# Window-attention scores with 49 weight columns in fixed PSUM banks, and the column transform in one piece per half

## The chip, the core and the metric

The kernel runs on one NeuronCore of one Trainium2 chip. Five engines work in parallel, each on its own queue: TensorE (PE, with its weight loads shown apart as PEld), VectorE (DVE), ScalarE (ACT), GpSimd (POOL) and SyncE (SP), which here issues nearly all DMA. The metric is device time in microseconds; a figure for a kernel is the median of its runs. PE writes its results to PSUM, which has eight banks of 128 partitions by 512 fp32 values; DVE and ACT read them from there.

## What is computed

Two layers on a batch of 32 images of 56 x 56 pixels and 128 channels, all in fp32. Each layer adds its result to its input and begins with a group norm (32 groups of 4 channels).

```python
# layer 0: shifted-window attention (windows of 7x7 = 49 tokens, 4 heads of 32)
xs  = roll(gn(x), (-3, -3)); win = windows(xs)              # 64 windows of 49 tokens
q, k, v = split(win @ w_qkv.T); q = q * 32 ** -0.5
attn = softmax(q @ k.T + relative_bias + shift_mask)         # 49 x 49 per head
x = x + roll(unwindow((attn @ v) @ w_proj.T + b_proj), (3, 3))

# layer 1: a Fourier mixer and a feed-forward part
h = gn(x)
xy = idct(einsum(dct(h along w)[:32 modes], w0))             # the rows
xx = idct(einsum(dct(h along h)[:32 modes], w1))             # the columns
x = x + relu((xx + xy) @ W1 + b1) @ W2 + b2
```

## The kernel before

**Cycles.** An image has eight rows of windows. The main loop runs over cycles; each handles one window row of attention, and beside it one step of the Fourier layer of an earlier image. `CONV_BEGIN` is 11: the Fourier layer of an image begins eleven cycles after its attention. Inside a cycle the Fourier step is called c. The order on PE, ACT, DVE and POOL is the order in which the Python code records the instructions (`manual_schedule`); the order on SP is chosen by the scheduler. The first eleven cycles (`first_rows`) have attention alone.

**A steady cycle on PE**, in order: q and k of the window row (L116, through `halved`), a part of the feed-forward input (L116) or of the mixing (L763), the product of the attention weights with v for the row three cycles back (L557, "AV"), a transform of the Fourier layer (L716) where one is due, the scores (L486), the inverse transforms (L802), v (L464), the feed-forward output (L116), and the projection (L602). Scores: for each of four pairs of windows, two pairs of heads and two windows of the pair, one matmul in a 64 x 64 tile of the array. Its weights are q of a window with 64 columns, that is the 49 tokens of the window and 15 that follow; its moving operand is k of two heads, 98 columns. An fp32 matmul stands as two records in the trace. The results lie at partitions 0 and 64 of two banks, one for each pair of heads. DVE adds bias and mask on the way out (L494), finds the maximum (L504), POOL subtracts it, ACT takes the exponential (L511). DVE and ACT empty the AV product (L587, L589).

**PSUM.** `attn_bank` hands out a new tile each time, with the tags pa0 to pa3 in turn, each with one buffer; `conv_bank` hands out new tiles with the tag pc and four buffers. A new tile may be written once all users of the tile before it in the same buffer are done.

**Columns.** The transform along the columns (`transform` with width false) takes tokens that `load_columns` (L745) reads back from a scratch tensor in DRAM, in groups of seven column pairs (`CH`), each group in two DMAs of 56 partitions (one per parity), in a buffer `htok` of which there are two. Groups 0 and 1 are loaded at c = 0, groups 2 and 3 at c = 1 behind the first transform; the transforms are due at c = 1 and c = 2, each with two groups of 224 columns per matmul. The transform along the rows (width true, at c = 0) reads x1 in SBUF, 448 columns per matmul. DVE transposes the results (`turn_modes`, L731).

**Other names.** L151 loads a quarter of the next image in four pieces, L339 to L344 transpose it on DVE; L225 forms bias plus mask (`bm`) at the start, from small tables that POOL loads; L773 stores mixed modes; L820 and L825 empty the inverse transforms.

Of the kernel before, what the change touches and what calls it, by code (L numbers as in the profile page):

```python
# [10 lines left out]
F32 = mybir.dt.float32  # L11
# [4 lines left out]
P = 128  # L16
S = 56
C = 128
# [4 lines left out]
WT = WS * WS  # L23
# [11 lines left out]
JP = 64  # L35
HB = 512

HALVES = (slice(0, P // 2), slice(P // 2, P))
# [10 lines left out]
def swin_fourier_kernel(  # L49
# [20 lines left out]
    nc = tc.nc  # L70
# [4 lines left out]
    work = ctx.enter_context(tc.tile_pool(name="work", bufs=2))  # L75
# [4 lines left out]
    def bank(tag, bufs):  # L80
        return psum.tile([P, HB], F32, tag=tag, name=tag, bufs=bufs)

    turns = count()

    def attn_bank():
        return bank(f"pa{next(turns) % 4}", 1)

    def conv_bank():
        return bank("pc", 4)

# [98 lines left out]
    with nc.allow_non_contiguous_dma(reason="relative position bias, once"):  # L191
# [4 lines left out]
        for ix in range(WS):  # L196
            src = bass.AP(
                rpb_rev.tensor, rpb_rev.offset + WS - 1 - ix, [[span, NH * span], [1, WS]]
            )
# [38 lines left out]
    for ps in LINE:  # L238
        r = ps.start
# [64 lines left out]
    def attn_buffer(r):  # L304
        return a_sb[r % 3 if r < CONV_BEGIN + 4 else r % 2]
# [167 lines left out]
    def attn_scores(im, i, r):  # L473

        q, a = q_sb, attn_buffer(r)

        ps = [attn_bank(), attn_bank()]  # L480
        for pr in range(NP):
            for hp in range(2):
                cs = HALVES[hp]
                for e in range(2):
                    w = 2 * pr + e
                    nc.tensor.matmul(  # L486
                        ps[hp][HALVES[e], pr * 2 * WT : (pr + 1) * 2 * WT],
                        lhsT=q[cs, w * WT : w * WT + JP],
                        rhs=k_sb[cs, :, w],
                        start=True,  # L490
                        stop=True,
                    )
        for hp in range(2):
            nc.vector.tensor_tensor(  # L494
                a[:, 2 * hp : 2 * hp + 2, :, 0:WT].rearrange("p u w j -> p w u j"),
                ps[hp][:, :RT].rearrange("p (w u j) -> p w u j", u=2, j=WT),
                bm[:, i // (NWR - 1), hp],
                ALU.add,
            )
# [43 lines left out]
    def attn_values(im, i, r, both=False):  # L543


        v = v_sb[r % 3]
        po = [attn_bank(), attn_bank()]
        if not both:
            po.reverse()
        HALF = RT // 2  # L550
        po4 = [p[:, :HALF].rearrange("p (r n s) -> p n r s", r=WS, s=WS) for p in po]
        eT = im.eT.pop(i)
        for pr in range(NP):
            for h in range(NH):
                for u in range(2):
                    ks = slice(u * JP, u * JP + WT)
                    nc.tensor.matmul(  # L557
                        po4[u][h * HD : (h + 1) * HD, pr],
                        lhsT=v[ks, pr, h * HD : (h + 1) * HD],
                        rhs=eT[ks, h * NP + pr, :WT],  # L560
                        start=True,
                        stop=True,
                    )

        if i % 2 == 0:
            im.oT = oT_sb[i // 2 % 2]
        oT = im.oT


        oTr = oT[:, i % 2 * RT : (i % 2 + 1) * RT].rearrange("p (r x) -> p r x", x=S)  # L570
        for u in (0, 1) if both else (1, 0):
            src = po[u][:, :HALF].rearrange("p (r f x) -> p r f x", r=WS, f=NP)
            n = NP - u
            dst = bass.AP(
                oTr.tensor,
                oTr[:, :, SS + u * WS :].offset,
                [oTr.ap[0], [S, WS], [2 * WS, n], [1, WS]],
            )
            parts = [(dst, src[:, :, :n])]
            if u:  # L580
                parts += [
                    (oTr[:, :, S - WS + SS :], src[:, :, n, : WS - SS]),
                    (oTr[:, :, 0:SS], src[:, :, n, WS - SS :]),
                ]
            for d, f in parts:
                if u and not both:
                    nc.vector.tensor_scalar(d, f, im.bias[:, 2:3], None, ALU.add)  # L587
                else:
                    nc.scalar.activation(d, f, AF.Identity, bias=im.bias[:, 2:3])  # L589
# [44 lines left out]
    def attn_squares(im, i):  # L634

        n0, n1 = WS * i // 2, WS * (i + 1) // 2
        piece = x1[:, n0:n1]
        im.sq = im.xr.pop(i)[:, : n1 - n0]
        nc.scalar.activation(im.sq, piece, AF.Square, scale=valid)
# [60 lines left out]
    CH = 7  # L700

    def transform(im, width, h):

        if width:
            toks = [x1[:, 2 * CH * h : 2 * CH * (h + 1)]]
        else:
            toks = [im.cols.pop(2 * h + j) for j in range(2)]
        dct_sb = (dct_w if width else dct_h)[:, :, 0]
        py = [conv_bank(), conv_bank()]
        at = 0  # L710
        for tok in toks:
            n = tok.shape[1] * KB
            for g in range(C // KB):
                cs = slice(g * KB, (g + 1) * KB)
                for r, ps in enumerate(LINE):
                    nc.tensor.matmul(  # L716
                        py[r][cs, at : at + n],
                        lhsT=dct_sb[ps],
                        rhs=tok[ps, :, cs],
                        start=True,  # L720
                        stop=True,
                    )
            at += n
        im.py[width, h] = py

    def turn_modes(im, width, h, r):

        p = im.py[width, h][r]
        t = work.tile([P, 4, C], F32, tag="z", name="modes", bufs=4)
        t = t.rearrange("p k c -> p (k c)")[:, : 2 * CH * KB]  # L730
        nc.vector.transpose(t, p[:, : 2 * CH * KB])  # L731
        im.modes.setdefault((width, h), []).append(t)

    def scale_modes(im, width, h, r):

        y = y_of[width][:, : NM * S].rearrange("p (k h n r) -> p h r n k", k=NM, h=2, r=2)[:, h]
        t = im.modes[width, h][r]
        nc.scalar.mul(y[:, r], t.rearrange("p (n k) -> p n k", k=NM), im.rstd)  # L738

    def shift_modes(im, width):  # L740

        y = y_of[width][:, :S]
        nc.scalar.activation(y, y, AF.Identity, bias=im.shift)

    def load_columns(im, g):  # L745

        t = work.tile([P, CH, C], F32, tag="htok", name="htok", bufs=2)
        src = im.scr.rearrange("h (n r) c -> r h n c", r=2)
        for r, ps in enumerate(LINE):
            nc.sync.dma_start(t[ps], src[r, :, CH * g : CH * (g + 1)])  # L750
        im.cols[g] = t

    def mix(im, width, g):

# [169 lines left out]
    def row(r):  # L924
        return (images[r // NWR], r % NWR) if 0 <= r < NB * NWR else (None, 0)

    def fourier(cycle):

        b, c = divmod(cycle - CONV_BEGIN, NWR)
        return [(images[b - k], c + k * NWR) for k in (1, 0) if 0 <= b - k < NB]  # L930
# [18 lines left out]
    def load_first(cycle):  # L949
        for im, c in fourier(cycle):  # L950
            if c == 0:
                load_columns(im, 0)
                load_columns(im, 1)

    def divide(cycle):
        if row(cycle - 1)[0]:
# [80 lines left out]
    def quarters(cycle):  # L1037
        def back():
            for im, c in fourier(cycle):
                for width, g in back_groups(c):  # L1040
                    modes_back(im, width, g)
                    if c < 8:
                        fetch_back(im, width, g)

        if not has_ff(cycle):
            back()
        im, i = row(cycle)
        if im:
            attn_scores(im, i, cycle)
        if has_ff(cycle):  # L1050
            back()

    def eighths(cycle):
        im, i = row(cycle - 3)
        if im:
            attn_values(im, i, cycle - 3, cycle % NWR in VALUES_BY_ACT)
            if cycle % NWR == NWR - 1:
                attn_squares(*row(cycle - 4))
        for im, c in fourier(cycle):
            if c == 0:  # L1060
                for h in range(2):
                    transform(im, True, h)
                    for r in range(2):
                        turn_modes(im, True, h, r)
                next(im.stats)
            if c == 1:
                for r in range(2):
                    scale_modes(im, True, 1, r)
                shift_modes(im, True)
            if c in (1, 2):  # L1070
                transform(im, False, c - 1)
                if c == 1:
                    for g in range(2):
                        load_columns(im, g + 2)

    def last_fetch(cycle):
        for im, c in fourier(cycle):
# [280 lines left out]
```

## Time and profile before

| | us |
|---|---|
| median of 3 runs | 3254.74 |
| the runs | 3251.01, 3254.74, 3256.28 |
| the profiled execution | 3245.75 |
| its span, first to last instruction | 3244.0 |
| mean granted TensorE clock in it | 0.988 of full speed |

The page's costliest groups of PE and their busy time in the profiled execution:

| group | what | records | busy us |
|---|---|---|---|
| L116, wff and hid | feed-forward output | 12288 | 714.1 |
| L116, xf and wff, 512 columns | feed-forward input | 2560 | 578.2 |
| L116, xw and wn | q and k | 2048 | 396.0 |
| L464 | v | 4096 | 291.2 |
| L602 | projection | 3584 | 246.4 |
| L486 | scores | 8192 | 236.2 |
| L557 | AV | 16384 | 208.6 |

A group's line in such a view reads: source line, engine, operation, output and inputs by the program's names, shapes (for PE the tile of the array and then partitions by moving columns), count, busy time, mean duration of one in ns, and the idle time before them with what ended it. Busy time is the union of the durations[...]; the difference between the starts of two matmuls is what the first one costs PE. In the view of one source line the three numbers are the least, median and greatest duration in ns. In the view of waits, a line has the total in us, the number of times and the longest. In the view in order of time, the first number is the start and the second the length, both in us.

### The profile page before, as it was taken

What the parts mean: (1) busy time and instruction counts of PE and PEld (TensorE: products, weight loads), DVE (VectorE), ACT (ScalarE), POOL (GpSimd) and SP (SyncE); (2) the same over time, 40 slices, a digit from 0 to 9 for tenths busy, and PEclk for the clock granted to TensorE, in tenths of its full rate; (3) what the DMA queues carried; (4) which work ended last, traced back from release to release, by engine and by line L of the source; (5) the groups of instructions that cost most, each with busy time, mean ns of one, the idle gap of its engine ahead of it and who ended that gap; (6) DMA issues with size and microseconds to landing.
All of it is one profiled execution on the core that took longest, in us unless ns stands there. A gap on an engine that the chain in (4) does not pass through costs nothing. (4 is left out here: it accounts for less than half of the span.)

```text
span 3244.0 us, 151708 instructions
## 1 busy us (share of the span) xinstructions
PE 3136.1 (97%) x65664; PEld 2363.2 (73%) x65664; DVE 2538.4 (78%) x4787; ACT 2165.5 (67%) x3959; POOL 2343.1 (72%) x2634
## 2 busy tenths in 40 slices
PE   5689999999999999999999999999999999999999
PEld 3467777777777777777777777777777777777776
DVE  8778887878887878888888887878888877887741
ACT  3466776666777666667676776666776666677663
POOL 7777777777777777777777777777777777777741
PEclk8789999999999999999999999999999999999999
DMA  6545556655566656566656556655666656565453
GB/s 113 111 116 147 142 139 145 137 142 139 140 146 146 141 142 144 134 143 148 142 140 147 139 142 145 140 141 144 142 141 148 138 145 144 134 145 139 119 143 96
DMA packets 1173439, 448.46 MB, mean 138 GB/s; under 512 B 529482, under 2 KB 1142908, under 8 KB 1172772
## 3 DMA queue, kind: packets, MB, share of 16 engines
q1 hardware_dynamic: 1163428, 433.22, 56.3%
q8 instruction: 516, 8.45, 1.1%
q10 hardware_dynamic: 8736, 5.38, 0.7%
q14 instruction: 151, 1.24, 0.1%
q0 software_dynamic: 608, 0.17, 0.0%
HBM read 277.00 MB, written 161.48 MB: 135 GB/s over the span
## 5 line engine op out<-in xcount | busy, mean ns | idle before, releaser
L530 POOL TENSOR_TENSOR blocks<-a,rs 128x512 f32<-128x512 f32 x1506 | 1280.0, 857 | 415.1 <-DVE rs L518 291.3
L116 PE MATMUL pc<-xf,wff 128*64 128x512 f32 (+2 forms) x3584 | 714.2, 539 | 1.8 <-DVE xf L820 1.6
L116 PE MATMUL pc<-wff,hid 128*64 128x128 f32 x12288 | 714.1, 273 | 1.7 <-ACT hid L847 1.0
L116 PEld LDWEIGHTS pc<-wff,hid 128*64 128x64 f32 x12288 | 680.4, 137 | 10.3 <-ACT hid L847 5.3
L505 POOL TENSOR_TENSOR a<-a,mx 128x784 f32<-128x784 f32 x251 | 377.7, 1505 | 285.6 <-DVE mx L504 270.2
L116 PEld LDWEIGHTS pc<-xf,wff 128*64 128x64 f32 x3584 | 266.0, 136 | 370.0 <-issue 274.8
L847 ACT ACTIVATE hid<-pc,b1sb 128x512 f32<-128x512 f32 (+2 forms) x896 | 500.5, 643 | 40.9 <-PE pc L116 40.8
L116 PE MATMUL pa<-xw,wn 128*64 128x392 f32 x2048 | 396.0, 501 | 29.8 <-ACT wn L417 29.8
L471 ACT COPY v<-pa 128x512 f32<-128x512 f32 x256 | 151.9, 593 | 349.1 <-PE pa L464 346.2
L494 DVE TENSOR_TENSOR a<-pa,bm 128x392 f32<-128x392 f32 x502 | 260.0, 559 | 152.8 <-PE pa L486 141.6
L451 ACT ACTIVATE k<-pa,bqkv,heads 128x392 f32<-128x392 f32 x512 | 318.9, 674 | 14.7 <-PE pa L116 0.6
L540 DVE STREAM_TRANSPOSE eT<-blocks 128x1024 f32<-128x1024 f32 x256 | 314.2, 1227 | 0.9 <-POOL blocks L530 0.9
L852 POOL TENSOR_TENSOR res<-res,b2sb 128x512 f32<-128x512 f32 (+1 forms) x224 | 252.7, 1128 | 85.1 <-DMA res<-scr 70.8
L438 ACT ACTIVATE q<-pa,bqkv 128x392 f32<-128x392 f32 x256 | 149.8, 585 | 242.6 <-PE pa L116 240.9
L130 POOL TENSOR_TENSOR xr<-xr,bproj 128x384 f32<-128x384 f32 (+1 forms) x256 | 293.0, 1144 | 25.0 <-DMA xr<-in_x_dram 10.5
L738 ACT ACTIVATE y<-modes,rstd 128x448 f32<-128x448 f32 x256 | 276.6, 1137 | 42.9 <-DVE modes L731 31.9
L464 PE MATMUL pa<-wn,xw 128*64 128x128 f32 x4096 | 291.2, 284 | 7.1 <-issue 3.3
L511 ACT ACTIVATE a<-a 128x784 f32<-128x784 f32 x251 | 214.7, 856 | 118.4 <-POOL a L505 118.3
L557 PEld LDWEIGHTS pa<-eT,v 49*32 49x32 f32 x16384 | 173.1, 106 | 161.1 <-issue 63.9
L516 DVE TENSOR_REDUCE sm<-a 128x16 f32<-128x784 f32 x251 | 241.3, 961 | 54.9 <-ACT a L511 54.1
L602 PE MATMUL pa<-wproj,oT 128*64 128x128 f32 x3584 | 246.4, 276 | 20.7 <-DVE oT L587 20.5
L464 PEld LDWEIGHTS pa<-wn,xw 128*64 128x64 f32 x4096 | 227.5, 140 | 45.5 <-ACT oT L589 8.1
(112 smaller groups left out, 4915.1 us busy)
## 6 DMA issues: line engine op xcount, KB each, us to landing
zscr<-z SPq DMA_DIRECT2D x512, 112.0 KB
xin<-in_x_dram SPq DMA_DIRECT2D x496, 112.0 KB
htok<-scr SPq DMA_DIRECT2D x256, 196.0 KB
zT<-zscr SPq DMA_DIRECT2D x192, 256.0 KB
res<-scr SPq DMA_DIRECT2D x160, 256.0 KB
out_dram<-res SPq DMA_DIRECT2D x160, 256.0 KB
scr<-x SPq DMA_DIRECT2D x256, 112.0 KB
xr<-in_x_dram SPq DMA_DIRECT2D x256, 84.0 KB
```

Of the source, the lines that this page charges most:

```text
L116: nc.tensor.matmul(dst[ps], lhsT=lhsT[:, ps], rhs=rhs, start=start, stop=stop)
L130: nc.gpsimd.tensor_tensor(piece, piece, bproj.unsqueeze(1).to_broadcast([P, n, C]), ALU.add)
L451: nc.scalar.activation(k_sb[:, u], pk[:, :RT].rearrange("p (w j) -> p w j", j=WT), AF.Identity, bias=im.bias[:, 3 + u : 4 + u], scale=head ...
L464: nc.tensor.matmul(pv[HALVES[w % 2], w // 2 * C : (w // 2 + 1) * C], lhsT=im.half[i // NP][:, t0 : t0 + JP], rhs=im.w[:, 2 * C : 3 * C], s ...
L494: nc.vector.tensor_tensor(a[:, 2 * hp : 2 * hp + 2, :, 0:WT].rearrange("p u w j -> p w u j"), ps[hp][:, :RT].rearrange("p (w u j) -> p w u ...
L505: nc.gpsimd.tensor_tensor(a3, a3, mx.unsqueeze(2).to_broadcast([P, 2 * NWR, WT]), ALU.subtract)
L530: nc.gpsimd.tensor_tensor(dst[to, k, :, :n], a3[src, :, kb * KB : kb * KB + n], rs[src].unsqueeze(2).to_broadcast([src.stop - src.start, 2 ...
L540: nc.vector.transpose(eT.rearrange("p t (k j) -> p k t j", k=2), blocks[r % 2])
L602: nc.tensor.matmul(pp[hs, (n - n0) * C : (n - n0 + 1) * C], lhsT=oT[:, t0 : t0 + JP], rhs=wproj, start=True, stop=True,)
L738: nc.scalar.mul(y[:, r], t.rearrange("p (n k) -> p n k", k=NM), im.rstd)
L847: nc.scalar.activation(hf[:, :n], ph[:, :n], AF.Relu, bias=b1sb[:, f : f + 1])
L852: nc.gpsimd.tensor_tensor(im.res[:, :k], im.res[:, :k], b2sb.unsqueeze(1).to_broadcast([P, k, C]), ALU.add,)
```

## The change

The eight PSUM banks become eight tiles that are allocated once, `attn_banks` and `conv_banks`, and are used in turn. The four of attention are cleared by a memset at the start. The score matmuls take 49 columns of q as weights in place of 64 and write 49 partitions at 0 and at 64; the other partitions of the two banks keep what an earlier use left there. DVE, POOL and ACT still handle all 128 partitions, and no later step uses those rows. The columns are loaded with one call of `load_columns` per half, fourteen column pairs, in a single buffer of twice the size, and each half's transform uses 448 columns per matmul. The line numbers of the changed kernel are higher by six in most of the code (scores L492, transform L722).

```diff
@@ -81,12 +81,18 @@
         return psum.tile([P, HB], F32, tag=tag, name=tag, bufs=bufs)
 
     turns = count()
+    attn_banks = [bank(f"pa{i}", 1) for i in range(4)]
+    for t in attn_banks:
+        nc.vector.memset(t, 0.0)
 
     def attn_bank():
-        return bank(f"pa{next(turns) % 4}", 1)
+        return attn_banks[next(turns) % 4]
+
+    conv_turns = count()
+    conv_banks = [bank(f"pc{i}", 1) for i in range(4)]
 
     def conv_bank():
-        return bank("pc", 4)
+        return conv_banks[next(conv_turns) % 4]
 
 
 
@@ -484,8 +490,8 @@
                 for e in range(2):
                     w = 2 * pr + e
                     nc.tensor.matmul(
-                        ps[hp][HALVES[e], pr * 2 * WT : (pr + 1) * 2 * WT],
-                        lhsT=q[cs, w * WT : w * WT + JP],
+                        ps[hp][e * JP : e * JP + WT, pr * 2 * WT : (pr + 1) * 2 * WT],
+                        lhsT=q[cs, w * WT : (w + 1) * WT],
                         rhs=k_sb[cs, :, w],
                         start=True,
                         stop=True,
@@ -704,7 +710,7 @@
         if width:
             toks = [x1[:, 2 * CH * h : 2 * CH * (h + 1)]]
         else:
-            toks = [im.cols.pop(2 * h + j) for j in range(2)]
+            toks = [im.cols.pop(h)]
         dct_sb = (dct_w if width else dct_h)[:, :, 0]
         py = [conv_bank(), conv_bank()]
         at = 0
@@ -742,13 +748,13 @@
         y = y_of[width][:, :S]
         nc.scalar.activation(y, y, AF.Identity, bias=im.shift)
 
-    def load_columns(im, g):
-
-        t = work.tile([P, CH, C], F32, tag="htok", name="htok", bufs=2)
+    def load_columns(im, h):
+
+        t = work.tile([P, 2 * CH, C], F32, tag="htok", name="htok", bufs=1)
         src = im.scr.rearrange("h (n r) c -> r h n c", r=2)
         for r, ps in enumerate(LINE):
-            nc.sync.dma_start(t[ps], src[r, :, CH * g : CH * (g + 1)])
-        im.cols[g] = t
+            nc.sync.dma_start(t[ps], src[r, :, 2 * CH * h : 2 * CH * (h + 1)])
+        im.cols[h] = t
 
     def mix(im, width, g):
 
@@ -950,7 +956,6 @@
         for im, c in fourier(cycle):
             if c == 0:
                 load_columns(im, 0)
-                load_columns(im, 1)
 
     def divide(cycle):
         if row(cycle - 1)[0]:
@@ -1070,8 +1075,7 @@
             if c in (1, 2):
                 transform(im, False, c - 1)
                 if c == 1:
-                    for g in range(2):
-                        load_columns(im, g + 2)
+                    load_columns(im, 1)
 
     def last_fetch(cycle):
         for im, c in fourier(cycle):
```

## The prediction

> **What bounds the kernel now.** I read the page's busy shares first, then the busy times in three stretches, then PE's waits, then the order of PE's blocks inside one cycle, and last the durations of the instructions that the change touches.
>
> ```profile
> PE 3136.1 (97%) x65664; PEld 2363.2 (73%) x65664; DVE 2538.4 (78%) x4787; ACT 2165.5 (67%) x3959; POOL 2343.1 (72%) x2634
> ```
> ```profile
> core 0: us, PE busy (x) PEld busy (x) DVE busy (x) ACT busy (x) POOL busy (x), PEclk, DMA share, GB/s
> 250.00:3100.00 2850.00, 2835.00 (x60172) 2145.06 (x60172) 2300.18 (x4310) 1979.15 (x3635) 2129.56 (x2373) 1.00 0.59 141
> 0.00:250.00 250.00, 164.27 (x3280) 120.23 (x3280) 199.68 (x403) 120.29 (x215) 182.78 (x227) 0.85 0.56 115
> ```
> ```profile
> PE pc L802 <- issue: 8.1, 12, 1.6
> PE pa L464 <- issue: 3.3, 7, 0.7
> PE pc L763 <- issue: 1.0, 2, 0.6
> PE pc L116 <- issue: 0.3, 1, 0.3
> ```
> From 250 to 3100 us PE is busy for 2835.0 of 2850 us, and the waits of PE in that stretch (last fence) come to 12.7 us, none of them for a buffer or a load. A busy PE can hide small waits[...]. So I also took the start times of single matmuls and compared like block changes with their own fast tenth: all the lateness in the stretch sums to 31 us. The kernel is bound by the rate at which PE streams; DVE, ACT and POOL have a fifth to a third of their time free. Only what shortens PE's stream, or makes PE wait, counts.
>
> One cycle of that stream, PE in order of time:
> ```profile
> 1506.01 0.81 PE L557 MATMUL pa<-eT,v 49*32 49x49 f32 x64
> 1506.64 1.11 PE L716 MATMUL pc<-htok,dct_h 56*32 56x224 f32 x32
> 1507.68 0.90 PE L486 MATMUL pa<-k,q 64*64 64x98 f32 x32
> 1508.52 1.09 PE L464 MATMUL pa<-wn,xw 128*64 128x128 f32 x16
> ```
> Each row is one block; the difference of two starts is what a block costs: columns 1.04 us, scores 0.84 us. The first four score matmuls, then all from the second round on, then the first matmuls of L557:
> ```profile
> L486 PE MATMUL pa<-k,q x4: 295/295/296, 1507.7 to 1507.7; 64*64 64x98 f32 x4
> ...
> L486 PE MATMUL pa<-k,q x32: 242/243/296, 1507.7 to 1508.3; 64*64 64x98 f32 x32
> ...
> L557 PE MATMUL pa<-eT,v x8: 227/228/228, 1506.0 to 1506.1; 49*32 49x49 f32 x8
> ```
> The first round takes 295 ns, the others 242 to 243: only the first weight load of a score block is in the open, for 53 ns. Later rounds start 84 ns apart, which is the matmuls' own time; their loads lie under the round before.
>
> [...] 53 ns at 64 columns above, and at 32 columns (L557) 228 less the later 203, that is 25 ns. [...] between blocks of different tile shapes the next matmul starts about 70 ns before the modelled end of the last (133 of 203 ns after L557, 172 of 243 ns after L486). [...]
>
> **The change, part by part.**
>
> *Narrower score weights.* 8192 loads go from 64 to 49 columns; the 98 moving columns stay. Rounds 2 to 8 are held by the matmuls (84 ns), so a shorter load below them gives nothing. The open first load gives 53 x 15/64 = 12.4 ns. There are 256 blocks (32 images of 8 rows): 256 x 12.4 = 3.2 us less. Bounds: 0, if the load is not priced by columns there; 3.2 at most, since the rest is hidden.
>
> *Column transform in one piece per half.* 2048 matmul records of 224 columns become 1024 of 448. The streamed columns are the same. Per transform, four rounds of 188 ns become two of 375 ns: 752 against 750. The row transform already has 448:
> ```profile
> L716 PE MATMUL pc<-htok,dct_h 56*32 56x224 f32 x2048 | 72.4, 358 | 0.0
> L716 PE MATMUL pc<-x,dct_w 56*32 56x448 f32 x1024 | 59.8, 555 | 0.0
> ```
> The 12.6 us between these rows is no saving: the row transform's two halves follow each other and drain once per image, the column halves drain twice. From starts, four row rounds and their drain take 1.75 us, so two take 1.75 - 0.75 = 1.00 us against 1.04 us now: at best 64 x 0.04 = 2.6 us. The 0.125 us between the first and second column matmul (wait for the loads) stays in both. I take half, 1.3 us; bounds 0 and 2.6.
>
> *Column loads.* 256 loads of 196 KB become 128 of 392 KB; 128 issues of some 0.45 us leave SP's queue. There is one buffer in place of two, so the second half's loads wait for all of the first transform. In the trace that wait ends at the same place in the queue now: the four loads go out at 1508.05, right behind the last column matmul. They land a median of 5.2 us after issue; the next transform starts a median of 3.2 us after the last landing. I cost it at nothing; that slack is the cover. Behind the load on SP stand image loads (L151), whose transposes already wait for DMA (39.1 us of DVE idle at L339): free time of DVE, not of PE.
>
> *Fixed banks.* In the built programs the turn through the banks is the same and PE's order is the same. What goes are 739 waits of PE for PE's own earlier matmuls, with 449 stand-alone wait instructions (51 ns each in the trace). What do they cost? Like block changes with and without such a wait: scores to L802, 65 ns and 65 ns; L802 to L464, 186 and 186. So I take 0; bound 449 x 51 ns = 22.9 us. What comes: 583 more wait instructions on DVE and 248 on ACT, for the other reader of the same bank. Each such reader had finished before PE could write the bank, so they are met already; on a busy DVE, instructions with one wait ahead follow as closely as those without (-81 against -76 ns median overlap). Bound, with all 583 in the open at 50 ns: +29 us.
>
> *Start and order.* Four memsets of 128x512 on DVE, some 0.55 us each (L494 is 559 ns for 392), 2.2 us, lie in front of this gap:
> ```profile
> 1.34 0.36 DVE L298 MEMSET heads<- 32x1 f32 x4
> 5.38 1.09 DVE L339 STREAM_TRANSPOSE xw<-y 128x512 f32<-128x512 f32 x1 [3.68 <-DMA y<-in_x_dram]
> ```
> The 3.68 us hide them. On POOL, the memset of bm (1.42 us) and smaller ones move ahead of the bias loads, about 2.4 us. DVE's bias sums (24, 4.74 us) start at 23.77; begun 1.5 us later they still end before the first scores at 30.68. On SP, one of an image's sixteen L151 pieces moves behind four stores (1530.2 to about 1536); its transpose comes at 1552.2.
>
> *Sum.* -3.2 - 1.3 = -4.5 us. Against the profiled execution's own 3245.75 us (span 3244.0, 1.75 around it) that is 3241.2. That execution lies 9 us under the median of the runs, 3254.74, and below all three; carried to the median: 3250.2 us.
>
> **Rivals.**
> B, faster: PE's wait instructions do take issue time. For it: L557's 64 pairs slow from 7 to some 17 ns apart in the second half of a block[...]. Against: equal gaps with and without. Half of the 22.9 us: 3250.2 - 11.5 = 3238.7.
> C, slower: the added waits on the readers lengthen the way from AV (L557) and scores back to PE. Place: L464 takes the bank that L587 or L589 has just emptied; after L802 it is late by 0.07 to 0.19 us on average in 88 of the cycles already. It decides once DVE comes to its PSUM reads idle (L494 waits for PE 117 times in the long stretch, 130.9 us), so that the wait instruction's 50 ns is in the open. Half of 29 us: 3250.2 + 14.6 = 3264.8.
> D, slower: the single column buffer. It decides when the second half lands over 3.2 us later than now; 4 us later costs about 0.8 us for each of 32 images, 26 us: 3276. Against: the same bytes, fewer issues.
> E, no effect: 49 columns load no faster than 64. Then only the 1.3 us is left: 3253.4.
>
> **Numbers.** A change under 0.2% (6.5 us) can't be told from none here. Forecast 0.44, E 0.08, B 0.27, C 0.15, D 0.06. Forecast and E fall within 0.2%, but for about 0.02 on the fast side. So faster 0.29, same 0.50, slower 0.21. The likeliest case alone: 3246 to 3255. The range reaches down to B's middle and up close to C's: 3238 to 3263.
>
> **What would show it.** Right: the first round of scores falls from 295 to about 283 ns with 243 after it; score blocks cost 0.72 in place of 0.73 us before L802; column blocks 1.00 to 1.04 us; PE still busy for 99% from 250 to 3100 us. B: gaps at same-shape block changes shrink, or L557's block does. C: PE gets waits on DVE or ACT at L464 or L116. D: PE waits for the column loads. The prediction fails if any of PE's block costs moves by 50 ns in all 256 cycles (12.8 us).

## The result and the profile after

The changed kernel takes 3244.86 us (median of 7 runs, 3242.93 to 3246.37); before, in the same job, 3254.53 us (3250.37 to 3256.28). The ratio is 0.997, interval 0.9961 to 0.9979: 9.7 us less. The forecast was 3250.2 us, 4.5 us less. The time lies in the range, but twice as much was gained as the sum says. The whole interval lies more than 0.2% under 1, which is the prediction's own line between faster and the same; it had held the same to be likelier. The profiled execution of the changed kernel took 3245.96 us (span 3244.2), close to its median.

The page's busy line, and the busy times in the long stretch (250 to 3100 us), of the changed kernel:

```profile
PE 3133.4 (97%) x64640; PEld 2334.7 (72%) x64640; DVE 2544.5 (78%) x4791; ACT 2164.4 (67%) x3959; POOL 2339.8 (72%) x2634
```
```profile
core 0: us, PE busy (x) PEld busy (x) DVE busy (x) ACT busy (x) POOL busy (x), PEclk, DMA share, GB/s
250.00:3100.00 2850.00, 2835.59 (x59260) 2120.40 (x59258) 2306.62 (x4312) 1980.49 (x3638) 2129.82 (x2376) 1.00 0.60 142
```
PE has 1024 matmuls and 1024 loads fewer, the columns' own, and is as busy as before. So far nothing shows a gain. One cycle of PE in order of time, and the first four score matmuls of it, then all 32:

```profile
1505.30 0.81 PE L563 MATMUL pa<-eT,v 49*32 49x49 f32 x64
1505.93 1.11 PE L722 MATMUL pc<-htok,dct_h 56*32 56x448 f32 x16
1506.97 0.89 PE L492 MATMUL pa<-k,q 64*49 64x98 f32 x32
1507.79 1.09 PE L470 MATMUL pa<-wn,xw 128*64 128x128 f32 x16
```
```profile
L492 PE MATMUL pa<-k,q x4: 282/282/283, 1507.0 to 1507.0; 64*49 64x98 f32 x4
...
L492 PE MATMUL pa<-k,q x32: 242/243/283, 1507.0 to 1507.6; 64*49 64x98 f32 x32
```
The first round fell from 295 to 282 ns, the others stay at 242 to 243: the weight term came as worked out. The score block costs 0.82 us in place of 0.84 before V, and the medians over all cycles say the same: 0.835 to 0.822 us before V (100 blocks), 0.727 to 0.714 before the inverse DCT (147). The column block still costs 1.04 us (medians 1.042 and 1.038).

The rest shows only when the time of whole images is taken, from one image's first `mean` matmul to the next one's. Of images 3 to 30 the quickest took 96.48 us before and 96.42 after. But within one execution images took up to 3.7 us more than the quickest before, and up to 2.4 us more in the changed kernel, and it is this that moved. The lines of waits that the prediction showed and passed over are the trace of it. PE's waits from 250 to 3100 us, changed kernel (us in total, times, longest):

```profile
PE pa L470 <- issue: 5.2, 8, 1.1
PE pc L808 <- issue: 4.8, 7, 1.0
PE pa L470 <- ACT oT L595: 1.6, 6, 0.3
PE pc L769 <- issue: 0.5, 1, 0.5
```
"Issue" says that PE waited for nothing that the profile shows as a releaser. So no buffer, load of data or reader of a bank is seen to hold it. What does, the experiments were made to find.

### The profile page after: what moved, and what is told of

Its sections match the earlier page's. It is cut to its first block, busy times and chain, and to the rows that moved or that the text cites. A ratio compares the mean times of both kernels' runs of the same rounds, so it can differ in the third digit from the quotient of the medians.

```text
span 3244.2 us, 149886 instructions
## 1 busy us (share of the span) xinstructions
PE 3133.4 (97%) x64640; PEld 2334.7 (72%) x64640; DVE 2544.5 (78%) x4791; ACT 2164.4 (67%) x3959; POOL 2339.8 (72%) x2634
## 4 chain that ended last, share of the span: by engine, by line
PE 88%; DVE 4%; ACT 3%; DMA 2%; issue 2%; SPq 1%; POOL 0%; ACTq 0%; DVEq 0%; POOLq 0%
PE pc L122 40%; PE pa L122 10%; PE pa L470 8%; PE pa L608 6%; PE pa L492 5%; PE pc L769 5%; PE pc L808 5%; PE pa L563 5%; PE pc L722 3%; DMA xin<-in_x_dram 2%; ACT z L777 1%; ACT k L457 1%; ACT xr L645 0%; PE pc L886 0%; DMA y<-in_x_dram 0%
## 5 line engine op out<-in xcount | busy, mean ns | idle before, releaser
L470 PE MATMUL pa<-wn,xw 128*64 128x128 f32 x4096 | 291.6, 284 | 12.1 <-issue 5.2
L563 PEld LDWEIGHTS pa<-eT,v 49*32 49x32 f32 x16384 | 173.6, 106 | 161.4 <-issue 68.4
L470 PEld LDWEIGHTS pa<-wn,xw 128*64 128x64 f32 x4096 | 227.6, 140 | 53.9 <-ACT oT L595 9.9
```

What stands on the lines that cost most here:

```text
L470: nc.tensor.matmul(pv[HALVES[w % 2], w // 2 * C : (w // 2 + 1) * C], lhsT=im.half[i // NP][:, t0 : t0 + JP], rhs=im.w[:, 2 * C : 3 * C], s ...
L563: nc.tensor.matmul(po4[u][h * HD : (h + 1) * HD, pr], lhsT=v[ks, pr, h * HD : (h + 1) * HD], rhs=eT[ks, h * NP + pr, :WT], start=True, sto ...
```

## The experiments

Twelve runs in three jobs, each job on another chip with the kernel before beside it. The ratios are to that kernel's runs in the same job, whose medians were 3250.31, 3251.56 and 3253.13 us; a ratio is not exactly that of the two medians.

**First job: the parts, one by one.** The same program again (one empty line added); the fixed banks alone; fixed banks with memsets and 49 columns, but columns in two pieces; the one-piece columns alone.

> The kernel before once more, without an edit, to have a second profile of it on the chip on which the parts are run. Every theory: ratio 1.000, interval within 0.1%. If the profile before was a quick execution by chance, the new span lies some 6 to 9 us above 3244; then the parts of the stream that are longer show where the 9.7 us are.

> Fixed banks alone: 64 weight columns, column loads in two pieces. PE's waits for itself go (739 to 0), its stand-alone wait instructions fall from 908 to 428, DVE's rise from 887 to 1413. Stream theory (waits of PE cost nothing): 0 us, within 1.5. Theory that waits take PE's issue time: -5 to -7 us, the part of the 9.7 us that weights and columns leave. Theory that the readers' waits cost: slower, +3 us or more.

```diff
...
-        return bank(f"pa{next(turns) % 4}", 1)
+        return attn_banks[next(turns) % 4]
...
-        return bank("pc", 4)
+        return conv_banks[next(conv_turns) % 4]
```

> Fixed banks, the four memsets and 49 weight columns; column loads in two pieces as before. Stream theory: -3.2 us, all of it from the open first weight load. Theory that waits take issue time: -8.5 to -10 us, about the whole change. If the columns carry the rest: -3 to -4 us only.

```diff
-                        ps[hp][HALVES[e], pr * 2 * WT : (pr + 1) * 2 * WT],
-                        lhsT=q[cs, w * WT : w * WT + JP],
+                        ps[hp][e * JP : e * JP + WT, pr * 2 * WT : (pr + 1) * 2 * WT],
+                        lhsT=q[cs, w * WT : (w + 1) * WT],
```

> Columns in one piece per half alone; pool banks and 64 weight columns. Stream theory: 0 to -2.6 us, rather 0, since the trace of the changed kernel has 1.038 us for a column block against 1.042. Theory that the columns carry the rest of the gain (128 fewer issues, other order on SP): -5 to -6 us.

```diff
-            toks = [im.cols.pop(2 * h + j) for j in range(2)]
+            toks = [im.cols.pop(h)]
...
-        t = work.tile([P, CH, C], F32, tag="htok", name="htok", bufs=2)
+        t = work.tile([P, 2 * CH, C], F32, tag="htok", name="htok", bufs=1)
```

| kernel | us | ratio, interval |
|---|---|---|
| before again | 3252.24 | 1.0001, 0.9992 to 1.0009 |
| fixed banks alone | 3245.39 | 0.9984, 0.9976 to 0.9992 |
| fixed banks, 49 columns | 3243.70 | 0.9976, 0.9967 to 0.9984 |
| one piece alone | 3245.33 | 0.9984, 0.9977 to 0.999 |

The repeated kernel's profile has a span of 3251.1 us, 7.1 us above the profile of before: that one was a quick execution. Fixed banks alone gain 5 us, and one piece alone gains 5 us, yet no block of PE's stream is shorter in the first, and only by 4 ns in 64 places in the second. Gains that come without any shorter block, from two edits that have nothing in common, called for a cause that both share. Both change the number of PE's instructions.

The profile of the repeated kernel shows where PE stood still. PE in order of time, with the idle time before a row in brackets:

```profile
741.41 0.90 PE L486 MATMUL pa<-k,q 64*64 64x98 f32 x32
742.14 0.75 PE L802 MATMUL pc<-idctw,zT 64*64 64x112 f32 x22
744.20 0.59 PE L802 MATMUL pc<-idctw,zT 64*64 64x112 f32 x10 [1.32 <-issue]
744.73 1.09 PE L464 MATMUL pa<-wn,xw 128*64 128x128 f32 x16
```
A group of 32 like matmuls, for which the profile shows no missing data, breaks off after 22 for 1.32 us. The queue list of the page gives the other half:

```profile
q8 instruction: 516, 8.45, 1.1%
```
These 516 packets have 16,384 bytes each. In the trace PE has 65,664 loads and 65,664 matmuls, with 908 stand-alone wait instructions and three drains 132,239 records; that is 516.6 blocks of 256. The changed kernel has 129,742, 506.8 blocks:

```profile
q8 instruction: 507, 8.31, 1.2%
```
In all fourteen traces the number of packets of q8 is within one of PE's records divided by 256, while q14, the other queue of instructions, has 152 on the repeated kernel's page. So q8 fetches PE's own instructions, 256 in a packet.

Counting every record of PE from the start, all 25 idle stretches of over 200 ns in the repeated kernel, from 250 to 3100 us, begin at instruction 192 of a block of 256. At each, a packet of q8 began 2.2 to 3.1 us before PE went on and ended 1.2 to 1.7 us before. In the changed kernel it is 16 of 20; the four others are in front of L470, where PE waits for ACT (the third line of its waits). The packets ahead of the repeated kernel's stalls were no slower than the rest: a median of 1.10 us for both.

The same floor shows at every packet, not only at the stalls. Number the packets from 1, and count PE's records in the order of their starts, from 0 and without the drain that opens the list: in none of the fourteen traces, with 506 to 516 packets each, did PE start record 256 m + 192 less than 1.09 us after packet m had landed, or less than 2.2 us after it had begun. The record just before starts as early as 0.18 us ahead of the landing in the repeated kernel. The packets there began with some 50 to 300 records left to that place, some 110 in the median at the stalls. AV, scores and inverse DCT are 320 records and take 3.09 us when nothing holds them (shown below), so 110 of them last about 1.1 us (an estimate from these two figures), half of the 2.2.

So theory F: PE waits for its own instructions where that place of a block comes behind a stretch of short instructions that PE runs through faster than the next packet comes (AV, scores and inverse DCT). Of the repeated kernel's 25 stalls 10 are at the inverse DCT (L802) and 10 at V (L464), which follows it or the scores. Among the long matmuls of q and k and of the feed-forward input (256 to 512 columns) the place fell 41 times from 250 to 3100 us in the profile of before and 41 times in that of the changed kernel, and at none of these was PE idle for over 200 ns. Call the number of an image's first `mean` matmul within a block of 256 the place at which the image starts. An image of the kernel before has 4132 instructions, 36 more than 16 blocks, so each image starts 36 places further, and after seven images nearly where it began. Both executions of that program had their stalls in the same images: those that start at places 10 to 18 took 98.4 to 100.2 us, those at 86 to 162 took 96.5 to 96.6. With 4054 instructions the changed kernel goes back by 42 per image. Times of images 3 to 30 of the changed kernel by the place at which they start:

```
place           images   mean us   from     to
97 to 179          10     96.56    96.42    96.81
180 to 211          5     96.76    96.45    97.12
212 to 33           9     97.76    97.17    98.43
34 to 96            4     98.10    97.60    98.79
```
The rival, theory S: the edits shorten the stream by themselves (fewer waits to issue, fewer products), and places have no effect.

**Second job: the place held, and the count undone.**

> The changed kernel with ten 512-column products of each image's feed-forward done as 2x256 columns (TensorE then has 4094 instructions for an image instead of 4054; 4096 is 16 blocks of 256) and 39 one-column products into an unused bank at the very start. Nothing else differs. So every image begins at nearly the same place of the 256-instruction blocks in which TensorE's instructions are fetched: image 3 at 157, image 31 at 101, where the changed kernel's images took 96.4 to 96.5 us each. Theory F (TensorE waits for its own instructions when a block ends inside the stretch of short products): all images 96.4 to 96.6 us, the 'issue' waits of the short products gone, about 20 us less than the changed kernel: 3222 to 3232 us. Theory S (the gain is only in the stream: fewer waits to issue, shorter weight loads; where the blocks lie is without effect): no quicker than the changed kernel, 3245 to 3252 us, for work was added.

> The same kernel with 5 instead of 39 one-column products at the start, 136 instructions fewer, so that image 3 begins at place 21 of a block and image 31 at 221. Theory F: images at such places took 97.2 to 98.4 us in the changed kernel, mean 97.8, so 1.4 us more for each of 28 images: 35 to 50 us more than the other locked kernel, 3255 to 3275 us, though 34 products fewer are run. Theory S: the same time as the other locked kernel within 2 us.

```diff
-            halved(ph[:, :n], wff1[:, f * P : (f + 1) * P], xff[:, t0 : t0 + n])
+            step = n // 2 if f == 0 and g < 5 else n
+            for c0 in range(0, n, step):
+                cols = slice(t0 + c0, t0 + c0 + step)
+                halved(ph[:, c0 : c0 + step], wff1[:, f * P : (f + 1) * P], xff[:, cols])
...
+        pz = conv_bank()
+        for _ in range(39):
+            nc.tensor.matmul(pz[:1, :1], lhsT=valid, rhs=valid, start=True, stop=True)
```
The other locked kernel has 5 in place of 39. In both, taking `pz` also moves the turn of the four `conv_banks` on by one. Measured: 3224.49 us, ratio 0.991 (0.9895 to 0.9925), against 3254.91 us, ratio 1.0007 (0.9999 to 1.0015). Thirty-four one-column products more at the start make the kernel 30.4 us faster. That is theory F; under S they should have been within 2 us. The size of the bad case was overrated (35 to 50 us were expected): its images 3 to 30 took 97.59 us in the mean, not 97.8, against 96.57 in the well placed kernel, and 28 times that difference is 28.5 of the 30.4 us. PE's waits in the long stretch, first the well placed kernel, then the badly placed one:

```profile
PE pa L470 <- ACT oT L595: 2.6, 9, 0.3
PE pa L669 <- DVE part L649: 0.3, 2, 0.2
PE pc L122 <- ACT xf L831: 0.3, 1, 0.3
```
```profile
PE pc L808 <- issue: 8.9, 15, 1.3
PE pa L470 <- issue: 5.3, 13, 0.8
PE pc L769 <- issue: 1.8, 4, 0.7
PE pc L122 <- issue: 0.9, 2, 0.5
```
"Issue" is gone from the first list and leads the second. The same step of a cycle, well placed and badly placed:

```profile
2145.90 0.81 PE L563 MATMUL pa<-eT,v 49*32 49x49 f32 x64
2146.64 0.89 PE L492 MATMUL pa<-k,q 64*49 64x98 f32 x32
2147.35 1.71 PE L808 MATMUL pc<-idctw,zT 64*64 64x112 f32 x64
2148.99 1.09 PE L470 MATMUL pa<-wn,xw 128*64 128x128 f32 x16
```
```profile
2160.95 0.81 PE L563 MATMUL pa<-eT,v 49*32 49x49 f32 x64
2161.68 0.89 PE L492 MATMUL pa<-k,q 64*49 64x98 f32 x32
2162.40 1.51 PE L808 MATMUL pc<-idctw,zT 64*64 64x112 f32 x54
2165.17 0.54 PE L808 MATMUL pc<-idctw,zT 64*64 64x112 f32 x10 [1.26 <-issue]
2165.64 1.09 PE L470 MATMUL pa<-wn,xw 128*64 128x128 f32 x16
```
From the start of L563 to that of L470 it is 3.09 us in one and 4.69 in the other, for the same work. The queues of the badly placed kernel from 2162.60 to 2163.55 us, just ahead of its pause:

```profile
q1 hardware_dynamic: 285, 0.14, 48.8%
q8 instruction: 1, 0.02, 5.8%
```
One packet of PE's instructions; it began 2.52 us before PE went on and ended 1.65 us before. In the badly placed kernel 33 of 35 idle stretches over 200 ns begin at instruction 192, in the well placed one none of 9.

> The changed kernel with 64 weight columns in the score products as before. It has as many TensorE instructions, at the same places of the blocks, as the changed kernel. The weight-load term alone: 256 score blocks x 12 to 14 ns = 3.1 to 3.6 us more than the changed kernel, about 3248 us. If 49 columns act otherwise (theory E of the prediction: loads no faster where it counts), less than 1 us.

The edit is the score diff above, undone. Measured: 3243.54 us, 0.9973 (0.9962 to 0.9983), beside 0.997 of the changed kernel in its own job. The 3248 us expected were not seen, but the total can't tell 3 us here, for the intervals are some 6 and 7 us wide. The blocks can: score blocks 0.835 and 0.727 us again, the quickest image 96.49 us in place of 96.42.

> The fixed banks alone (that run took 0.9984 of the time before), with four 512-column products of each image's feed-forward done as 2x256 columns, so that an image has 4133 TensorE instructions instead of 4117; before it has 4132. Theory F: the gain of the fixed banks came from where the blocks fall; with the count of before the gain goes: 0.9995 to 1.001 of before, about 3250 us. Theory S (739 fewer waits on TensorE's own matmuls, 449 fewer stand-alone wait instructions, save time by themselves): the gain of 5 us stays, 0.998 to 0.9988.

The split above, for `f == 0 and g < 2`. Measured: 3249.67 us, 0.9997 (0.9989 to 1.0005). With four products split in an image the gain of the fixed banks is gone as far as the intervals can say (they overlap from 0.9989 to 0.9992), so their 739 fewer waits bring nothing that shows. Its waits for "issue" at the inverse DCT are 7.8 us, with 5.8 in the unpadded kernel. The splits cost nothing: the quickest image took 96.51 us with and without them.

**Third job: the other part undone, and the change without stalls.**

> The columns in one piece alone (that run took 0.9984 of the time before), with 16 of the 512-column products of each image's feed-forward done as 2x256 columns: 4133 TensorE instructions for an image instead of 4069; before it has 4132. Theory F (fetch of TensorE's instructions): the gain goes, 0.9993 to 1.001 of before. Theory S (16 products fewer, and a column block that ends sooner, save time by themselves): 0.998 to 0.9988 stays.

The split here is for `(f == 0 and g < 5) or (f == 1 and g < 3)`. Measured: 3249.51 us, 0.9993 (0.9985 to 1.0001). By the ratios more than half of this gain goes; by the medians 3.6 of 5.0 us are left. So this run settles less than the last: the intervals overlap from 0.9985 to 0.9990, and sixteen splits are not free. The quickest image took 96.51 us with them and 96.48 without, and 32 times the unrounded 0.038 us is 1.2 us. The waits at the inverse DCT point to theory F, unpadded and then padded:

```profile
PE pc L802 <- issue: 3.1, 6, 1.2
```
```profile
PE pc L802 <- issue: 7.6, 10, 1.3
```

> The good locked kernel once more, to stand in the same job as the two below: 3221 to 3228 us, 0.991 of before.

Measured: 3224.10 us, 0.9913 (0.9899 to 0.9926), as the first time.

> The good locked kernel with 64 weight columns in the scores. With the fetch stalls out of both, the weight-load term stands alone: 147 score blocks that go straight into the inverse DCT lengthen by 13 ns (1.9 us, sure), the 100 before V by up to 13 ns (1.3 us): 2 to 3.3 us more than the good locked kernel, a ratio to before larger by 0.0006 to 0.001. If the loads are hidden where it counts: no difference.

Measured: 3228.09 us, 0.9922 (0.991 to 0.9935), 4.0 us more. The intervals overlap; the blocks of the trace settle 1.8 us of it, for the 147 blocks went from 0.714 to 0.726 us, and up to 1.3 us more in the 100 before V, which went from a median of 0.822 to 0.835.

> The kernel before with the columns in one piece (pool buffers and 64 weight columns as before), six products split and 36 one-column products at the start: 4093 TensorE instructions for an image, image 3 at place 172 of a block and image 31 at 88. Theory F: before, too, loses its stalls: images of 96.48 to 96.6 us, 3225 to 3230 us, and against the good locked kernel only the stream's terms are left: 2 to 3.3 us of weights and under 1 us of all else. If the fixed banks save time by themselves (theory S): 5 us or more above the good locked kernel.

```diff
+            step = n // 2 if f == 0 and g < 3 else n
...
+        for _ in range(36):
```
Measured: 3227.92 us, 0.9921 (0.9908 to 0.9935). The kernel with pool buffers and 64 columns, well placed, equals the fixed banks with 64 columns, well placed (3228.09), within intervals some 8 us wide. The quickest image took 96.49 us with pool buffers and 96.52 with fixed banks, so the fixed banks shorten no image. All that is left of PE's waits from 250 to 3100 us:

```profile
PE pa L464 <- ACT oT L589: 1.2, 5, 0.3
```

The version to keep is thus the changed kernel with ten split products and a start of 39 small ones: 0.991 and 0.9913 of before in its two jobs, where the change alone has 0.997.

## Why the prediction was half right

All its signs of being right came: 282 ns in the first round, 0.714 us before the inverse DCT, 1.038 us for the columns, PE busy for 99% of the long stretch. They test the stream's blocks, and most of the gain was not in the blocks. That 3244.86 us lies in the range is luck in part: the likeliest case alone was 3246 to 3255, the range reached down to 3238 for rival B, and B is not what happened.

- **Narrower weights, -3.2 us: right.** The open load fell by 13 ns (295 to 282) where 12.4 was estimated from the 53 ns at 64 columns, in proportion to the columns; 247 blocks at 13 ns are 3.2 us, and the well placed pair shows 4.0 with overlapping intervals.
- **One piece per half, -1.3 us: mis-sized.** Two rounds and a drain, that is the time from the last product's start to the next block, were to cost between 1.00 and 1.04 us; the block went from 1.042 to 1.038, so 64 x 0.004 = 0.25 us. The 1.00 was taken from the row transform, whose first two products start 0.017 us apart. In a column block they start 0.125 us apart, in one piece as in two; the prediction named that wait and yet left it out of the 1.00. So the last product of two rounds starts at 0.572 us, where two rounds of rows have it at 0.537, and both need 0.466 us from there to the next block: 1.038 and 1.003.
- **Column loads, 0: right.** No wait of PE for `htok` appears; rival D is out.
- **Fixed banks, 0: right for the stream, wrong for the time.** Well placed, pool and fixed banks with 64 columns have medians 0.2 us apart (each interval is some 8 us wide), and the padded fixed banks have 0.9997: nothing of the size of B or C, 11.5 and 14.6 us. In the fixed banks alone, 480 wait instructions fewer (15 in an image) moved the places, and the kernel gained 5 us. B put the time at 3238.7 us, about as far under the measured one as the forecast lay above it, and for a reason that the padded run and the well placed pair rule out at that size.
- **The step that failed** is in the first part: "The kernel is bound by the rate at which PE streams", with PE's "issue" waits shown and read as "none of them for a buffer or a load". They were waits for PE's own instructions. The 31 us of lateness that the prediction found in the stretch were mostly of this kind (the well placed kernels keep 3 to 5 us in images 3 to 30, counted against the quickest image), and it took that lateness to be the same after. Missing from the sum was a term for how the change moves these places.
- **Its size.** In images 3 to 30 the lateness above the quickest image is 29.6 us in the repeated kernel and 21.8 in the changed one, 7.7 less; the quickest image itself gives 28 x 0.06 = 1.7 us. Together that is 9.4 us, near the 9.7 measured, though these are two single executions. The span differs by only 6.9, since the start and the tail took 2.5 us more in that profile. The profile of before that the prediction used had 24.2 us of lateness with the same program, 5.4 us less: its quickness, 9 us under the median, was largely luck with the same stalls. Set against it, the changed kernel has only 2.4 us less lateness.

What stays open: why one program's lateness differs by 5 us between two executions, why at the stalls 1.2 to 1.7 us pass between the landing of a packet and PE's going on, and why the place is 192 of this count; where a fetched block itself ends is not seen in the traces. How much lateness a count of 4054 would have was read from the traces, not derived beforehand.

## What to carry to other kernels

Where PE is bound by a long unrolled stream of short instructions, count its instructions per repeated unit modulo what a packet of its queue holds (256 in these traces), and look where the same place of the blocks falls; a few instructions more or fewer can be worth more than the edit that brings them (here 34 one-column products at the start were worth 30.4 us, the change 9.7). Take "issue" waits that recur in the midst of like instructions for a possible fetch until shown otherwise (8.9 us at the inverse DCT of the badly placed kernel, none in the well placed one), and time the repeated unit as well as its blocks. And before a gain of some 0.2% is credited to an edit, undo its change of the instruction count alone.

## What the runs showed of the hardware

PE's instructions came over q8 in packets of 16,384 bytes, 516 of them for 132,239 records in the repeated kernel and 507 for 129,742 in the changed one: 256 instructions in a packet. Most of this fetch was hidden: of the 472 blocks in the long stretch of the repeated kernel 25 had PE idle for over 200 ns at place 192. But the images' lateness, mostly these stalls and shorter ones, comes to 29.6 us, 0.9% of the kernel, with 1.4 us for the longest stall. A packet took a median of 1.1 to 1.2 us, and at every stall PE went on only 2.2 to 3.3 us after a fetch began; in no trace did it pass record 256 m + 192 less than 2.2 us after packet m began. Two such kernels that differ by 34 one-column products at the very start differ by 30.4 us.
